# A run-time branch moved from between two passes to the end of the kernel, where it runs a second pass of its own

## The chip, the cores and the metric

The kernel runs on one core of a Trainium2 chip. The metric is the time of one execution on the device in microseconds (us); lower is better. A core has five engines with an instruction stream each: TensorE (PE, matmuls and transposes), VectorE (DVE), ScalarE (ACT), GpSimd (POOL) and SyncE (SP). They meet only through semaphores. In this kernel SP issues the plain transfers between memory and the core, and POOL issues the indirect ones, which gather or scatter rows by a list of row numbers.

## The reference, cut to what matters

Two layers over 64 graphs of 256 nodes with 256 features each (16384 rows in all). The first layer is an attention over the adjacency matrix and a Mamba-2 block; the second is a relational graph convolution and a mixture of eight experts:

```python
x = x + _L0_gnn_ref(_layernorm(x), adj, L0_gnn_W, L0_gnn_a)
x = x + _L0_ffn_ref(_layernorm(x), L0_ffn_W_in, ...)            # Mamba-2
x = x + _L1_gnn_ref(_layernorm(x), L1_gnn_adj, adj, L1_gnn_weight, L1_gnn_bias)
x = x + _L1_ffn_ref(_layernorm(x), L1_ffn_gate_w, ...)          # experts
...
    masks = (relation[None] == rel_ids[:, None, None, None])    # relations 1 to 4
    h = jnp.einsum('rbnm,bmd->rbnd', masks, x)
    y = jnp.einsum('rbnd,rdo->bno', h, weight)
...
    idx = jnp.argmax(probs, axis=-1)                            # one expert per row
    pos = (jnp.cumsum(one_hot, axis=0) * one_hot).sum(-1) - 1   # place in its queue
    kept = pos < C                                              # C = 2560 rows
    hmid = relu(einsum('ecd,edf->ecf', buf, w1) + b1)           # 256 -> 1024
    ybuf = einsum('ecf,efd->ecd', hmid, w2) + b2                # 1024 -> 256
    y = nan_to_num(ybuf[idx, pos_g] * (prb * kept))
```

The adjacency matrix that is given holds only 0 and 1, so of the four relations only the first occurs. The kernel relies on that in its usual form, tests it, and has a general form for other matrices.

## The kernel before, in words

**Pass 1** goes through the graphs two at a time, in 32 groups of 512 rows. Each group does the attention, the Mamba-2 block and the graph convolution, writes its rows to `x3d` in device memory, chooses an expert for every row and scatters a record of four numbers per row (`slots`: row number, probability, and the two numbers of the layer norm) to the place of the row in its expert's queue. The steps of all groups are put in order by a planner written in the kernel (`Plan`), from a cost and a due time for each step, and stand in the program in that order. Two blocks of expert work (`first_block`) are planned into pass 1, to run beside its last groups in homes that the groups no longer need; their last four indirect stores of 128 rows (L1271) are the last work of pass 1.

**The test and the branch.** Each group adds up, on ACT, a number that exceeds a bound if an entry of the matrix is neither 0 nor 1 (`tested`). L1432 to L1438 make of these one whole number, `general`, with two DVE operations, a matmul and a copy. At L1440 every engine loads that number into a register, and at L1444 it enters or jumps over the general form of pass 1: a loop over pairs of groups that does the whole pass again with four relations. With the given data it is jumped over. An engine that jumps over such a block must then count its semaphores as if it had run it; POOL does that for its indirect transfers with an instruction of its own (INC_SWDGE_SEM).

**Pass 2** (`Blocks`, from L1461) does the other expert blocks: first those of 256 rows (the halves, `kind` 1), then those of 512 rows (the wholes, `kind` 0). How many of each there are is known at run time only, so the blocks stand in nested branches (L1602), and an engine leaves the nest after the last block that exists. A block needs its records (`fetch_slots`, SP, L1496), its expert's weights (`fetch_weights`, SP, four transfers, L1505 to L1514), the row numbers as whole numbers (`placed`, two small DVE operations, L1249 and L1250), its rows (`gather`, POOL, one indirect transfer per 128 rows, L1253), the norm (`normed`, DVE, L1259) and the transposes (`turned`, PE and ACT, L1539 and L1542). All this is done a block or two ahead; `experts` then does the two matmuls (L1565, L1575), and DVE, ACT and POOL finish and store the rows. Ahead of the first block `begin` does it for the halves and then for the wholes:

```python
def begin(self):
    for i in range(2):
        self.fetch_slots(i)
    self.fetch_weights(0)
    for i in range(2):
        self.gather(i)
    self.turned(self.norm(0), 0)
...
for blocks in (halves, wholes):
    blocks.begin()
```

So PE, in its own order, transposes the first block of the halves, the first block of the wholes, and then begins the first block of the halves. I call this stretch the prelude.

**Memory.** On-chip memory is given out in pools. `wts` holds pass 1's weights, about 26 KB per partition; `fast` lies above it and holds pass 1's work tiles, those of `first_block` among them. Both are closed before pass 2 opens `et`, `es` and, for PSUM, `eps`, which lie over their bytes. In `et` the homes of a kind come list by list: three of `meta`, of `place`, of `xg`, then two of each other.

Of the kernel before, what the change touches and what calls it, by code (L numbers as in the profile page):

```python
# [19 lines left out]
P = 128  # L20
# [267 lines left out]
def gnn_mamba_rgcn_moe(ctx: ExitStack, tc: tile.TileContext, a: dict, out: bass.AP):  # L288
# [10 lines left out]

    nc = tc.nc  # L300
# [89 lines left out]
    pass1 = ctx.enter_context(ExitStack())  # L390
    wts = pass1.enter_context(tc.tile_pool(name="wts", bufs=1))

    DG, DQ = D + E + 1, D + E + 1 + NH
    DA = DQ + 2
    WX = DA + E + 1 + NH  # L400
    wx = wts.tile([P, 2, WX], F32, name="wx")
    win = wts.tile([P, 2, DPROJ], F32, name="win")
    nc.scalar.dma_start(out=win, in_=a["L0_ffn_W_in"].rearrange("(k p) o -> p k o", p=P))
    wrel = wts.tile([P, 1, 2, DG], F32, name="wrel")
    gb = wts.tile([P, E], F32, name="gb")
    nc.scalar.dma_start(out=gb, in_=row(a["L1_ffn_gate_b"]).broadcast_to([P, E]))
    blin = wts.tile([P, DG], F32, name="blin")
    nc.scalar.dma_start(out=blin[:, 0:D], in_=row(a["L0_ffn_b_lin"]).broadcast_to([P, D]))
    brel = wts.tile([P, DG], F32, name="brel")
    nc.scalar.dma_start(out=brel[:, 0:D], in_=row(a["L1_gnn_bias"]).broadcast_to([P, D]))  # L410
    dtb = wts.tile([P, NH], F32, name="dtb")
    nc.scalar.dma_start(out=dtb, in_=row(a["L0_ffn_dt_bias"]).broadcast_to([P, NH]))
    aneg = wts.tile([P, NH], F32, name="aneg")
    nc.scalar.dma_start(out=aneg, in_=row(a["L0_ffn_A_log"]).broadcast_to([P, NH]))
    nc.scalar.activation(aneg, aneg, AF.Exp)
    nc.vector.tensor_scalar(aneg, aneg, -1.0, None, ALU.mult)
    dch = wts.tile([P, NCT], F32, name="dch")
    dskip = a["L0_ffn_D"].rearrange("(c q) -> q c", q=2)
    for q in range(2):
        nc.scalar.dma_start(  # L420
            out=dch[q * 64 : (q + 1) * 64, :], in_=dskip[q : q + 1, :].broadcast_to([64, NCT])
        )

    cw = wts.tile([P, NCT + 1, 4], F32, name="cw")
    nc.sync.dma_start(out=cw, in_=a["L0_ffn_conv_w"].rearrange("(c p) k -> p c k", p=P))
    nc.vector.tensor_scalar(cw, cw, 0.5, None, ALU.mult)
    cb = wts.tile([P, NCT + 1], F32, name="cb")
    nc.sync.dma_start(out=cb, in_=a["L0_ffn_conv_b"].rearrange("(c p) -> p c", p=P))
    nc.vector.tensor_scalar(cb, cb, 0.5, None, ALU.mult)
    wf = wts.tile([P, NCT, DG], F32, name="wf")  # L430

    gq = wx[:, :, DA:WX]

    def centred(pool, banks, dst, src, n):

        ps = banks.tile([P, 512], F32, tag="ps0", name="ps")
        for k in range(2):
            nc.tensor.matmul(
                ps[:, :n], lhsT=ones_pp, rhs=src[:, k, :], start=(k == 0), stop=(k == 1)
            )  # L440
        for k in range(2):
            nc.vector.scalar_tensor_tensor(
                dst[:, k, :], ps[:, :n], -1.0 / D, src[:, k, :], ALU.mult, ALU.add
            )

    def projected(pool, banks, dst, src, n):

        for k in range(2):
            ps = banks.tile([P, 512], F32, tag="ps0", name="ps")
            for o in range(2):  # L450
                nc.tensor.transpose(
                    ps[:, o * P : (o + 1) * P], src[:, k, o * P : (o + 1) * P], ident
                )
            srcT = pool.tile([P, 2 * P], F32, tag="srcT", name="srcT")
            nc.vector.tensor_copy(srcT, ps[:, : 2 * P])
            ps = banks.tile([P, 512], F32, tag="ps0", name="ps")
            for o in range(2):
                nc.tensor.matmul(
                    ps[:, :n], lhsT=srcT[:, o * P : (o + 1) * P], rhs=gq[:, o, :n],
                    start=(o == 0), stop=(o == 1),  # L460
                )
            nc.vector.tensor_copy(dst[:, k, :], ps[:, :n])

    def relation(pool, banks, dst, r):

        nc.sync.dma_start(
            out=dst[:, :, 0:D], in_=a["L1_gnn_weight"][r].rearrange("(k p) o -> p k o", p=P)
        )
        centred(pool, banks, dst[:, :, 0:D], dst[:, :, 0:D], D)
        projected(pool, banks, dst[:, :, D:DG], dst[:, :, 0:D], E + 1)  # L470

    with tc.tile_pool(name="prep", bufs=1) as prep, tc.tile_pool(
        name="prep_ps", bufs=2, space=PSUM
    ) as prep_ps:
        own = prep, prep_ps

        w0 = prep.tile([P, 2, D], F32, name="w0")
        nc.sync.dma_start(out=w0, in_=a["L0_gnn_W"].rearrange("(k p) o -> p k o", p=P))
        gq0 = prep.tile([P, 2, E + 1 + NH], F32, name="gq0")
        nc.vector.memset(gq0[:, :, E : E + 1], 0.0)  # L480
        nc.sync.dma_start(
            out=gq0[:, :, 0:E], in_=a["L1_ffn_gate_w"].rearrange("(k p) e -> p k e", p=P)
        )
        nc.vector.tensor_copy(gq0[:, :, E + 1 :], win[:, :, DPROJ - NH :])
        centred(*own, gq, gq0, E + 1 + NH)
        nc.vector.memset(gq[:, :, E : E + 1], -1.0 / D)
        centred(*own, wx[:, :, 0:D], w0, D)
        projected(*own, wx[:, :, D:DQ], wx[:, :, 0:D], E + 1 + NH)
        for o in range(0, DPROJ - NH, 512):
            part = win[:, :, o : min(o + 512, DPROJ - NH)]  # L490
            centred(*own, part, part, min(512, DPROJ - NH - o))
        relation(*own, wrel[:, 0], 0)
        for vec, dst in (("L0_ffn_b_lin", blin), ("L1_gnn_bias", brel)):
            col = prep.tile([P, 2], F32, tag="col", name="col", bufs=2)
            nc.sync.dma_start(out=col, in_=a[vec].rearrange("(k p) -> p k", p=P))
            ps = prep_ps.tile([P, 512], F32, tag="ps0", name="ps")
            for k in range(2):
                nc.tensor.matmul(
                    ps[:, : E + 1], lhsT=col[:, k : k + 1].to_broadcast([P, P]),
                    rhs=gq[:, k, : E + 1],  # L500
                    start=(k == 0), stop=(k == 1),
                )
            nc.vector.tensor_copy(dst[:, D:DG], ps[:, : E + 1])

        av = prep.tile([P, 2, D], F32, name="av")
        for i in range(2):
            nc.sync.dma_start(
                out=av[:, i, :],
                in_=a["L0_gnn_a"][i * D : (i + 1) * D, :].rearrange("d o -> o d").broadcast_to([P, D]),
            )  # L510
# [78 lines left out]
    def summed_up(ends):  # L589
        for e in range(1, E):  # L590
            nc.vector.tensor_add(ends[..., e : e + 1], ends[..., e : e + 1], ends[..., e - 1 : e])
# [1048 lines left out]
```

## Time and profile before

| What | Value |
|---|---|
| Median of 9 runs | 2527.13 us (2523.79 to 2534.23) |
| The profiled execution | 2528.44 us, its span 2526.6 us |
| Last matmul of pass 1 ends, first expert matmul of pass 2 begins | 1884.4 us, 1919.8 us |
| PE busy from 1884 to 1920 | 4.7 us (0.42 + 0.67 + 3.57) |
| Mean clock granted to PE, from 1895 to 1920 | 0.50 |
| Last store issued (POOL), end of the span | 2514.6 us, 2526.6 us |

Times in the profile are microseconds from the start of the span. A row of a timeline gives the start, the duration, the engine, the line and the operation, then the tile that is written and those that are read; in brackets stands how long the engine had been idle and what ended that. An engine with a q behind its name (POOLq) is the sequencer of that engine: branches, register loads and waits. Rows with slashes are for all instructions of one kind on a line: shortest, median and longest in ns, then the first and the last start. The releaser in brackets is worked out from semaphores, and where a wait is for several it can be the wrong one.

### The profile page before, as it was taken

The numbers are of one execution on the slowest core, as the hardware profiler recorded it, in microseconds if no ns is written. First come the engines' busy times: TensorE is split into PE (matmuls) and PEld (weight loads), VectorE is DVE, ScalarE is ACT, GpSimd is POOL, SyncE is SP. The second block draws the span as 40 slices with busy tenths as digits, with TensorE's granted clock in tenths as the row PEclk, the third lists the DMA queues.
The fourth block names the chain that finished last, engine by engine and source line by source line (L and its number), as shares of the span: only waits on it lengthen the run. The fifth ranks groups of instructions, "written<-read, shape, count | busy, mean of one in ns | idle before, by whom it ended". The sixth has DMA issues, their size and how long they took to land. (4 is left out here: it accounts for less than half of the span.)

```text
span 2526.6 us, 34990 instructions
## 1 busy us (share of the span) xinstructions
PE 2384.9 (94%) x11489; PEld 1661.8 (66%) x11489; DVE 1921.4 (76%) x4811; ACT 1642.5 (65%) x3712; POOL 832.6 (33%) x756
## 2 busy tenths in 40 slices
PE   5899999999999999999999999999886999999997
PEld 4567766666667666766766676666655666666665
DVE  3899999999989999999999999999752344334433
ACT  1878887878888888888888888786522223322232
POOL 1122424333343433334343333432523222322222
PEclk8999999999999999999999999999997999999999
DMA  3212222322222322222232222231416333333333
GB/s 113 45 23 55 60 61 63 79 56 54 62 54 70 68 66 54 62 53 70 57 75 56 53 62 58 66 62 40 136 38 212 119 109 128 110 124 103 111 124 69
DMA packets 170175, 194.66 MB, mean 77 GB/s; under 512 B 24855, under 2 KB 154975, under 8 KB 169968
## 3 DMA queue, kind: packets, MB, share of 16 engines
q1 hardware_dynamic: 121184, 131.24, 16.6%
q0 software_dynamic: 47104, 59.14, 12.8%
q8 instruction: 97, 1.59, 0.3%
q10 hardware_dynamic: 1680, 1.79, 0.2%
q14 instruction: 110, 0.90, 0.1%
HBM read 108.27 MB, written 45.97 MB: 61 GB/s over the span
## 5 line engine op out<-in xcount | busy, mean ns | idle before, releaser
L697 PE MATMUL ps<-xnT,win 128*128 128x512 f32 x1152 | 544.4, 602 | 4.0 <-ACT xnT L739 4.0
L916 DVE SCALAR_TENSOR_TENSOR y<-ps,cw,y 128x510 f32<-128x510 f32 (+2 forms) x480 | 351.1, 739 | 6.6 <-ACT y L909 5.0
L983 ACT ACTIVATE dm<-ps,cs 128x256 f32<-128x256 f32 (+1 forms) x1024 | 334.5, 477 | 22.8 <-PE ps L697 22.4
L705 POOL TENSOR_TENSOR rs<-ve,mhalf 128x4 f32<-128x4 f32 x96 | 164.4, 1713 | 559.1 <-DVE ve L703 435.8
L697 PEld LDWEIGHTS ps<-xnT,win 128*128 128x128 f32 x1152 | 205.4, 191 | 171.7 <-issue 159.4
L1565 PE MATMUL ps<-xnT,w 128*128 128x512 f32 (+1 forms) x704 | 289.4, 570 | 4.0 <-DMA meta<-slots 4.0
L1575 PE MATMUL ps<-w,hid 128*128 128x256 f32 x1312 | 290.4, 379 | 0.0
L1575 PEld LDWEIGHTS ps<-w,hid 128*128 128x128 f32 x1312 | 247.6, 190 | 40.9 <-issue 9.1
L697 PE MATMUL ps<-wf,gate 128*128 128x265 f32 x1024 | 252.0, 388 | 0.5 <-DVE gate L1061 0.5
L1565 PEld LDWEIGHTS ps<-xnT,w 128*128 128x128 f32 x704 | 136.0, 193 | 146.1 <-issue 133.4
L1041 DVE TENSOR_TENSOR dm<-dm,bc 128x1536 f32<-128x1536 f32 x128 | 225.6, 1764 | 1.7 <-ACT dm L989 0.2
L1569 ACT ACTIVATE hid<-ps,b 128x512 f32<-128x512 f32 (+1 forms) x176 | 115.8, 658 | 166.7 <-PE ps L1565 165.7
L697 PEld LDWEIGHTS ps<-wf,gate 128*128 128x128 f32 x1024 | 191.4, 190 | 48.5 <-issue 11.2
L1580 DVE TENSOR_TENSOR yv<-ps,b 128x256 f32<-128x256 f32 x82 | 34.8, 425 | 237.1 <-PE ps L1575 237.1
L1048 PE MATMUL ps<-dm,xdt 128*64 128x256 f32 x1024 | 169.5, 397 | 33.5 <-DVE dm L1041 33.0
L989 ACT ACTIVATE dm<-dm 128x1536 f32<-128x1536 f32 x128 | 198.6, 1554 | 0.0
L1271 POOL DMA_INDIRECT out_dram<-yf,place x82 | 81.3, 992 | 343.1 <-DVE yf L1588 337.6
L1235 POOL DMA_INDIRECT slots<-meta,sl x128 | 127.9, 1000 | 195.2 <-DVE sl L1232 149.1
L1581 ACT ACTIVATE yv<-yv,meta 128x256 f32<-128x256 f32 x82 | 41.7, 508 | 183.3 <-DVE yv L1580 183.3
L713 DVE BATCH_NORM_STATS2 st<-x 128x6 f32<-128x256 f32 x384 | 151.6, 413 | 7.4 <-DMA x<-in_x_dram 6.8
L922 ACT ACTIVATE xh<-y 128x512 f32<-128x512 f32 x160 | 101.0, 631 | 75.1 <-DVE y L916 66.1
L697 PE MATMUL ps<-wh,eT 128*128 128x273 f32 x512 | 142.6, 407 | 5.6 <-ACT eT L835 4.9
(298 smaller groups left out, 5018.7 us busy)
## 6 DMA issues: line engine op xcount, KB each, us to landing
w<-in_L_ffn_w_dram SPq DMA_DIRECT2D x48, 1024.0 KB
x<-blin POOLq DMA_DIRECT2D x32, 530.0 KB
x<-brel POOLq DMA_DIRECT2D x32, 530.0 KB
adji<-in_adj_dram SPq DMA_DIRECT2D x32, 512.0 KB
x<-in_x_dram SPq DMA_DIRECT2D x32, 512.0 KB
x3d<-x SPq DMA_DIRECT2D x32, 512.0 KB
out_dram<-x SPq DMA_DIRECT2D x32, 512.0 KB
cm<-bm SPq DMA_DIRECT2D x32, 128.0 KB
```

The lines of the kernel that those rows point to most:

```text
L697: nc.tensor.matmul(out_, lhsT=lhsT, rhs=rhs, start=(i == 0), stop=(i == len(pairs) - 1))
L705: s.step(POOL, 1.0, lambda: nc.gpsimd.tensor_tensor(rs(), ve(), mhalf[:, 0:4], ALU.pow), [ve], [rs])
L713: s.step(DVE, 0.34, lambda j=j: nc.vector.bn_stats(sb()[:, j, :], src()[:, j, 0:D]), [(src, j)], [(sb, j)])
L916: nc.vector.scalar_tensor_tensor(y3[:, :, d:], p3[:, :, : N - d], cw[:, c, k : k + 1], y3[:, :, d:], ALU.mult, ALU.add,)
L983: nc.scalar.activation(dm()[:, q, bi, o : o + n], ps()[:, t0 + N - n : t0 + N], AF.Relu, bias=cs()[:, j, h : h + 1], scale=-1.0,)
L989: s.step(ACT, 1.38, lambda: nc.scalar.activation(dm(), dm(), AF.Exp, scale=-1.0), [], [dm])
L1041: s.step(DVE, 1.67, lambda dm=dm: nc.vector.tensor_mul(dm(), dm(), bc().unsqueeze(1).to_broadcast([P, 2, 2, N + P])), [bc], [dm])
L1048: nc.tensor.matmul(o, lhsT=xdt()[:, 2 * bi, h * 64 : (h + 1) * 64], rhs=dm()[:, q, bi, 0:N], start=True, stop=False,)
L1235: s.step(POOL, 1.1, lambda j=j: apart("slots", nc.gpsimd.indirect_dma_start(out=slots, out_offset=bass.IndirectOffsetOnAxis(ap=sl()[:, j : ...
L1565: nc.tensor.matmul(ps[:, :n], lhsT=w1[:, k, f * P : (f + 1) * P], rhs=xnT[:, k, :], start=(k == 0), stop=(k == 1),)
L1569: nc.scalar.activation(hid[:, f, :], ps[:, :n], AF.Relu, bias=self.b1[i % 2][:, f : f + 1])
L1575: nc.tensor.matmul(ps[:, :D], lhsT=hid[:, f, j * P : (j + 1) * P], rhs=w2[:, f, :], start=(f == 0), stop=(f == NFT - 1),)
```

## The change

The two passes become functions of a form, `first_pass(form, pass1)` and `second_pass(form, pass2)`. The usual form (`fast`) runs both without a branch between them. After it every engine loads `general`, and enters or jumps over the general form (`slow`), which now holds the preparation of the weights, the loop, and a second pass of its own. With the given data it is jumped over as before.

In the second pass four things differ. The homes are made block by block: all of the halves' block 0 first, then the other homes of its blocks 1 and 2, then those of the wholes, so that the halves' first homes lie on the bytes of `wts`. The prelude goes step by step over both kinds instead of kind by kind. Its row numbers are written by POOL, not DVE. The four operations that make `general` stand behind the prelude.

```diff
+                kinds = {
+                    "meta": (3, [P, J, 4], F32), "place": (3, [P, 2, J], I32), "xg": (3, [P, J, D], F32),
+                    "w1": (2, [P, 2, F], F32), "w2": (2, [P, NFT, D], F32), "b1": (2, [P, NFT], F32),
+                    "b2": (2, [P, D], F32), "xnT": (2, [P, 2, J * P], F32),
+                }
...
+                for i in range(3):
+                    for name, (n, shape, dtype) in kinds.items():
+                        if i < n:
+                            getattr(self, name).append(et.tile(
+                                shape, dtype, tag=f"{name}{kind}{i}", name=name, bufs=1))
...
-    for blocks in (halves, wholes):
-        blocks.begin()
+        both = (halves, wholes)
+        for blocks in both:
+            for i in range(2):
+                blocks.fetch_slots(i)
+        for blocks in both:
+            for i in range(2):
+                blocks.gather(i, nc.gpsimd)
+        for blocks in both:
+            blocks.fetch_weights(0)
+        for blocks in both:
+            blocks.turned(blocks.norm(0), 0)
+        if form == "fast":
+            other = es.tile([P, NG], F32, tag="yv", name="other")
+            nc.vector.tensor_scalar(other, tested, float(N) + 1.0, None, ALU.is_gt)
+            others = es.tile([P, 1], F32, tag="others", name="others", bufs=1)
+            nc.vector.tensor_reduce(others, other, AX.X, ALU.max)
+            ps = eps.tile([P, 512], F32, tag="ps", name="ps")
+            nc.tensor.matmul(ps[:, 0:1], lhsT=ones_pp, rhs=others, start=True, stop=True)
+            nc.vector.tensor_copy(general, ps[0:1, 0:1])
...
-    again = nc.values_load(
-        general[0:1, 0:1], min_val=0, max_val=P,
-        skip_runtime_bounds_check_because="a count of partitions",
-    )
-    with tc.If(again > 0), ExitStack() as slow:
...
-    pass1.close()
...
+    for form in ("fast", "slow"):
+        with ExitStack() as here:
+            if form == "slow":
+                again = nc.values_load(
+                    general[0:1, 0:1], min_val=0, max_val=P,
+                    skip_runtime_bounds_check_because="a count of partitions",
                 )
+                here.enter_context(tc.If(again > 0))
+            with ExitStack() as pass1:
+                first_pass(form, pass1)
+            with ExitStack() as pass2:
+                second_pass(form, pass2)
```

## The prediction

> **What bounds the kernel now.** I read the share of slices first, then the busy time by stage, then each engine's timeline across the place that changes, then the branch rows.
>
> ```profile
> PE 2384.9 (94%) x11489; PEld 1661.8 (66%) x11489; DVE 1921.4 (76%) x4811; ACT 1642.5 (65%) x3712; POOL 832.6 (33%) x756
> PE   5899999999999999999999999999886999999997
> ```
>
> TensorE is the bound everywhere except at the start, at the seam between the passes (tenths 8, 8, 6) and in the last slice. The branch sits in that seam. The PE timeline there:
>
> ```profile
> 1883.82 0.59 PE L1376 MATMUL ps<-xh,dm 128*128 128x256 f32 x2
> 1907.15 0.66 PE L1539 MATMUL ps<-ident,xn 128*128 128x128 f32 x2 [22.74 <-DMA meta<-slots]
> ...
> 1918.42 1.38 PE L1539 MATMUL ps<-ident,xn 128*128 128x128 f32 x4 [1.20 <-DVE xn L1259]
> 1919.78 5.46 PE L1565 MATMUL ps<-xnT,w 128*128 128x256 f32 x13
> ```
>
> Pass 1's last matmul ends at 1884.4 and the first expert matmul starts at 1919.8: 35.4 us with only twelve transposes. That is all this change can win here. POOL in the same stretch shows what fills it:
>
> ```profile
> 1890.48 0.97 POOL L1271 DMA_INDIRECT out_dram<-y,hide  x1 [1.43 <-DVE y L1390]
> 1898.72 1.01 POOL L1253 DMA_INDIRECT xg<-x3d,place  x1 [7.26 <-DVE place L1250]
> 1900.03 0.97 POOL L1253 DMA_INDIRECT xg<-x3d,place  x1 [0.30 <-issue]
> ...
> 1908.54 0.95 POOL L1253 DMA_INDIRECT xg<-x3d,place  x1 [5.02 <-DVE place L1250]
> ...
> 1912.29 0.94 POOL L1253 DMA_INDIRECT xg<-x3d,place  x1 [0.30 <-issue]
> ```
>
> The last store of pass 1 is issued at 1890.48. Then come the halves' four gathers, a hole of 5.02 us, and the wholes' gathers. The hole is DVE's: it stands in order behind the halves' normalising (first at 1906.43) before it writes the wholes' row numbers at 1908.03. PE has the wholes' transposes ahead of the first block, so the wholes' fourth gather (1912.29) is what releases the start. The rows of the branch itself:
>
> ```profile
> L1444 POOLq EVENT_SEMAPHORE  x5: 17/43/43, 1891.3 to 1893.5; - x5
> L1444 DVEq COMPARE_BRANCH  x1: 72/72/72, 1890.4 to 1890.4; - x1
> L1444 POOLq COMPARE_BRANCH  x1: 53/53/53, 1890.8 to 1890.8; - x1
> L1444 POOLq INC_SWDGE_SEM  x1: 1020/1020/1020, 1893.6 to 1893.6; - x1
> L1444 DVEq EVENT_SEMAPHORE  x1: 21/21/21, 1893.6 to 1893.6; - x1
> ```
>
> DVE's jump took 1890.4 to 1893.6, and POOL saw pass 1's last stores land at 1893.5. SP's first slot fetch follows at 1895.22. So the branch is not alone on this path: the landing of the stores ends at the same moment.
>
> **Does the new pass wait for those stores too?** This decides the sum. Pass 2's tiles lie over two closed pools: the weights (`wrel`'s last matmul is at 1832.8) and the work tiles, whose last reader is the store at 1890.48. The only other place where a pool opens over a closed one is the start:
>
> ```profile
> 42.98 0.38 SPq L549 DMA_DIRECT2D b1d<-b1t  x1
> ...
> 45.35 0.64 POOL L573 MEMSET blank<- 128x640 f32 x1 [40.65 <-DMA b1d<-b1t]
> ```
>
> `blank` is the first tile of the new pool and `b1t` the last of the old one, yet it waited 40.65 us for the landing of `b1t`. A new pool's tile there waited for all users of the pool below, not for those of its own bytes. I take the same for pass 2, over both pools: then the new order of the homes frees nothing early, and all of the prelude still starts at 1893.5.
>
> **The change part by part**, under that reading.
>
> 1. *Branch, its loads and joins out of the seam.* SP no longer waits for DVE's join, loads its register and works through its waits after it: the first slot fetch goes from 1895.22 to about 1893.65, -1.55 us.
> 2. *New prelude order.* SP issues four slot fetches at its old pace (0.85 us apart), so the first weights leave at 1897.0 as they did (1896.94) and cost nothing; by the DMA packets they had landed at about 1906.5, so they are next if the gathers end before that. Row numbers are written by POOL: a POOL copy of 128x8 took 0.25 us (L1190), so a pair 0.5, plus the 0.3 that POOL shows between its own issues. Slot fetch to row numbers took 2.27 (1895.22 to 1897.49). Chain: 1893.65 + 2.27 + 0.8 = 1896.7 first gather; at 1.28 a gather and 0.8 a pair the wholes' fourth is issued at 1896.7 + 7 x 1.28 + 2 x 0.8 - 2 x 0.3 (the gap is in both) = 1906.6, against 1912.29: -5.7, the 1.55 of part 1 included. The four DVE copies removed were idle time.
> 3. *Landing.* Fourth gather to its normalising took 6.35 (1918.64), then 1.14 to the first expert matmul. DMA was full there (share 1.02 from 1908 to 1920), so I keep 6.35. Low bound: were bytes the limit, only the earlier start counts, -1.55. High bound: pass 1's gather landed in 4.85 (issue 1771.33, normalising 1776.18), and -5.7 becomes -7.2; with DVE's price for the row numbers (0.33 a pair) -8. I take -5.7, the row of this very transfer. PE starts at 1914.1, and the rest of pass 2, bound by PE, moves with it. The slow first block (9.56 us where later ones take 7.07, granted clock 0.50 before it) stays, as PE still idles.
> 4. *The test of `general`* (four small instructions) moves from pass 1 into the wait of part 3: nothing. Without that cover, under 1 us. PE's 0.28 at 1869.78 stood beside a wait for ACT.
> 5. *The branch at the end.* PE, ACT, DVE and SP reach it early; POOL is last:
>
> ```profile
> L1602 POOLq EVENT_SEMAPHORE  x4: 17/43/43, 2517.1 to 2517.3; - x4
> ...
> L1602 POOLq COMPARE_BRANCH  x2: 43/46/50, 2514.3 to 2519.1; - x2
> ...
> L1602 POOLq INC_SWDGE_SEM  x1: 1667/1667/1667, 2517.4 to 2517.4; - x1
> ```
>
> Its leaving of the last nest took 2.8 us (2514.3 to 2517.1; DVE's also 2.8), the counter 1.67, and then a drain of 6.24 that ends the kernel. After that nest POOL now loads `general` (0.51 at L1440), jumps over the general form, makes up its semaphores (0.35) and its counter, and only then drains. The jump is unseen: low 0.5 (POOL over the old general form, 1890.8 to 1891.3), high 6.75 (PE's dearest, L1602). The skipped code now holds a whole second pass, as the code left at 2514.3 does, so I take 2.8. Sum 0.51 + 0.05 + 2.8 + 0.35 + 1.67 = +5.4; bounds 2.7 (with 0.5 and a counter of 1.02, and 0.3 for the return) and 9.7.
>
> [...]
>
> **Sum.** -5.7 + 5.4 = -0.3. The profiled execution took 2528.44 (span 2526.6 and 1.84 around it), 1.31 above the median 2527.13; -0.3 on the median is 2526.8. A difference under 0.2% (5.05 us) is about what a measurement of this kernel can't tell from no change.
>
> **Rivals.**
> - *A: a tile waits only for the pool under its own bytes.* The homes of the halves' first block fit over the weights (some 26 KB), so its slots, weights and gathers are done before 1885; SP and DMA are idle enough (34 GB/s from 1850 to 1900). Left after 1893.65 are the wholes' slots and four gathers: 1893.65 + 2.27 + 0.8 + 3 x 1.28 = 1900.6, + 6.35 + 1.14 = 1908.1. Seam -11.7, sum -6.3: 2520.8. For it: the homes are ordered to allow it. Against it: `blank`.
> - *A2: waits by bytes alone.* All of the prelude hides; PE starts at about 1889, after the last PSUM reader (1887.5), at a better clock. Seam -31 - 2.5, sum -28: 2499. Against it: the same row, harder.
> - *B, slower: the end's jump.* Place: POOL, ahead of the 6.24 drain. If it is fetched twice, to the block that makes up semaphores and back, at SP's price for leaving the nest (2484.7 to 2489.6, 4.9), the end costs 0.51 + 9.8 + 0.35 + 1.67 + 0.1 = 12.4, sum +6.7: 2533.8. It turns the sign from an end of 5.7, and passes 0.2% from 10.8. For it: nothing overlaps POOL's end. Against it: POOL's return took 0.4 (2519.1 to the drain at 2519.6).
>
> **How the numbers follow.** Likeliest case 0.58 (bounds: -8 + 2.7 = -5.3 to -1.55 + 9.7 = +8.2, so 2521.8 to 2535.3 of its own): 0.45 within 0.2%, 0.05 faster, 0.08 slower. A 0.19 and A2 0.07, faster. B 0.16: 0.14 slower, 0.02 within. Together faster 0.31, same 0.47, slower 0.22. The range 2516 to 2534.5 takes in A with its error, the likeliest case but its far corner and most of B; A2 and the rest of B, under 0.2, stay out.
>
> **What would show it.** Right: first slot fetch near 1893.6; POOL's gathers in one row with no hole of 5 us; first expert matmul near 1914; POOL's drain 5 us later after its last store than now (2519.6 against 2514.56). Wrong: gathers or weights of pass 2 among pass 1's last stores (A), expert matmuls by 1890 (A2), a gap above 8 us ahead of the drain (B). The prediction also falls if the wholes' fourth gather lands no sooner although issued sooner.

## The result, and the profile after

The kernel after takes 2537.45 us (median of 10 runs, 2531.86 to 2540.56), the kernel before, in 30 runs of the same comparison, 2527.19. The ratio is 1.0037, with a 95% interval of 1.0028 to 1.0046: 10.3 us slower. The prediction was 2526.8 with a range up to 2534.5, so it was wrong, in sign and in range.

The profiled execution of after took 2544.68 us (span 2542.8), 7.2 above its median; that of before 2528.44 (span 2526.6). The first two lines of its page, PE's busy time and PE's tenths in 40 slices:

```profile
PE 2397.0 (94%) x11489; PEld 1669.3 (66%) x11489; DVE 1921.3 (76%) x4803; ACT 1647.2 (65%) x3712; POOL 833.8 (33%) x764
...
PE   5999999999999999999999999999887999999996
```

PE has the same 11489 matmuls as before and is busy 12.1 us longer with them (2397.0 against 2384.9). That can't come from the seam or the tail, where it has almost nothing to do. The PE timeline across the seam (start, duration, line, tiles; in brackets the idle time before and what ended it):

```profile
1893.70 3.19 PE L1377 MATMUL ps<-xh,dm 128*128 128x256 f32 x14
1916.46 0.66 PE L1532 MATMUL ps<-ident,xn 128*128 128x128 f32 x2 [19.57 <-DVE xn L414]
...
1927.06 1.51 PE L1532 MATMUL ps<-ident,xn 128*128 128x128 f32 x4 [0.17 <-DVE xn L414]
1928.76 7.52 PE L1550 MATMUL ps<-xnT,w 128*128 128x256 f32 x26 [0.19 <-issue]
```

Pass 1 ends at 1896.89 instead of 1884.42. From there to the first expert matmul it is 31.87 us instead of 35.36. POOL in that stretch:

```profile
1902.95 0.97 POOL L426 DMA_INDIRECT out_dram<-y,hide  x1 [1.43 <-DVE y L1391]
1908.15 0.19 POOL L404 CAST place<-meta 128x2 int32<-128x2 f32 x1 [4.23 <-DMA meta<-slots]
...
1908.96 1.06 POOL L408 DMA_INDIRECT xg<-x3d,place  x1 [0.40 <-POOL place L405]
...
1912.19 1.02 POOL L408 DMA_INDIRECT xg<-x3d,place  x1 [0.17 <-POOL place L405]
...
1918.58 1.04 POOL L408 DMA_INDIRECT xg<-x3d,place  x1 [0.30 <-issue]
```

The gathers come in one row; the hole of 5.02 us is gone. The wholes' fourth gather leaves 15.63 us after pass 1's last store instead of 21.81. No part of the prelude starts before that store. The rows of the branch at the end (duration of one in ns: minimum, median, maximum; then the starts):

```profile
L1611 POOLq EVENT_SEMAPHORE  x6: 17/30/43, 2533.6 to 2534.0; - x6
...
L1611 POOLq COMPARE_BRANCH  x1: 55/55/55, 2530.6 to 2530.6; - x1
L1611 POOLq INC_SWDGE_SEM  x1: 1647/1647/1647, 2534.1 to 2534.1; - x1
```

POOL jumps at 2530.6, is at the other side at 2533.6, and then adds to its counter; 1.65 later comes a drain of 6.16 us (6.24 in before). From POOL's last store to the last drain, which follows that one and ends the kernel, it is 18.08 us, in before 11.80.

So the span of 2542.8 against 2526.6 divides thus: pass 1's end +12.5, the seam -3.5, pass 2's matmuls +0.9 (592.18 against 591.32), the tail (from the last matmul to the end) +6.3; together +16.2. Seam and tail are what the prediction was about, +2.8 by these two profiles. The 12.5 of pass 1, whose instructions did not change on any engine but for the four that make `general`, it had at nothing.

Where it lies: at 100 us after is 2.6 us early, and then it loses 1.3 to 2.4 us at a time at nine places, one or two pairs of groups (109 us each) apart. At each of these places, and at four others, PE waits 2.2 to 2.6 us for DVE's masked `dm`, in both kernels, thirteen times in pass 1. One of them in before, then the same one in after:

```profile
431.06 0.66 PE L1048 MATMUL ps<-dm,xdt 128*64 128x256 f32 x4 [2.50 <-DVE dm L1041]
...
429.19 0.66 PE L1084 MATMUL ps<-dm,xdt 128*64 128x256 f32 x4 [2.22 <-DVE dm L1077]
```

What follows differs. Three stretches of 3.41 us each of after, with such a gap from 426.97 to 429.19 (length, busy time of PE, PEld, DVE, ACT and POOL, the granted clock, DMA's share, GB/s):

```profile
426.87:430.28 3.41, 1.19 (x13) 1.02 (x14) 3.38 (x5) 1.25 (x5) 2.60 (x1) 1.00 0.00 0
430.28:433.69 3.41, 3.41 (x13) 2.32 (x9) 3.38 (x7) 2.75 (x5) 0.00 (x0) 0.50 0.89 307
433.69:437.11 3.42, 3.42 (x20) 2.39 (x19) 2.68 (x7) 3.05 (x7) 1.01 (x1) 1.00 0.02 5
```

And of before, where the same gap lies from 428.55 to 431.06:

```profile
426.22:429.63 3.41, 2.33 (x10) 1.45 (x8) 2.80 (x7) 2.12 (x7) 0.67 (x2) 1.00 0.01 1
429.63:433.05 3.42, 1.99 (x18) 1.68 (x19) 3.42 (x4) 2.09 (x7) 2.19 (x1) 1.00 0.24 84
433.05:436.46 3.41, 3.41 (x15) 2.49 (x14) 3.33 (x10) 3.41 (x5) 0.13 (x1) 1.00 0.67 228
```

In after the gap lies whole in one stretch (PE busy 1.19 of 3.41) and the next stretch runs at half the clock (0.50). In before it is shared by two stretches (2.33 and 1.99 busy) and the clock stays at 1.00. In the record of the granted clock in these two profiles all falls in pass 1 after 100 us begin on one grid of 3.41 us and last 3.41 or 6.83. I call one a spell, and a stretch of that grid a window. After eleven of the thirteen gaps a spell follows in after, after two in before (the first two expectations below count ten and one of twelve). Over pass 1 from 100 us on that is 47.8 us at half clock against 20.5. Taking half the clock for half the work, the difference would cost 13.7 us if PE were busy in all of it, an estimate from these two lengths; by the rows of after a matmul of 128x292 (L733) took 684 ns in the half-clock stretch above and 409 ns from 440 to 520 us.

Pass 1's matmuls are the same in both kernels, so they can be set side by side one by one. From 300 to 1660 us after falls back by 17.5 us. Of these, 13.1 come just behind the gaps: 1.35 to 1.47 at each of the nine places where after has a spell and before has none, and under 0.2 at each of the other four. Another 5.4 come just ahead of the gaps, 0.7 to 1.2 at each of five places where DVE waited 3.5 us for its inputs to `xdt`, instead of 2.5 to 2.9 as in before; the gaps themselves are 1.0 shorter. So half clock is three quarters of what this execution lost there, and the longer waits are the rest. Ahead of the gap above, DVE's waits in before and then in after:

```profile
424.93 0.69 DVE L1031 TENSOR_TENSOR xdt<-ps,dt 128x512 f32<-128x512 f32 x1 [1.36 <-PE ps L697]
426.37 0.69 DVE L1031 TENSOR_TENSOR xdt<-ps,dt 128x512 f32<-128x512 f32 x1 [0.75 <-PE ps L697]
...
427.83 0.69 DVE L1031 TENSOR_TENSOR xdt<-ps,dt 128x512 f32<-128x512 f32 x1 [0.43 <-PE ps L697]
...
420.74 0.69 DVE L1067 TENSOR_TENSOR xdt<-ps,dt 128x512 f32<-128x512 f32 x1 [0.59 <-PE ps L1062]
423.59 0.69 DVE L1067 TENSOR_TENSOR xdt<-ps,dt 128x512 f32<-128x512 f32 x1 [2.17 <-PE ps L733]
425.03 0.69 DVE L1067 TENSOR_TENSOR xdt<-ps,dt 128x512 f32<-128x512 f32 x1 [0.75 <-remote]
```

How busy PE was in the window ahead of a spell can be read from the profiles of all runs together. From 300 to 1665 us they hold 212 windows at full clock in which PE is busy for less than 2.6 us. All 85 with at most 1.39 us busy are followed by half clock, none of the 109 with 1.58 or more, and 8 of the 18 between (1.49 went both ways). This holds for these gaps only: near 1700 us, where PE does other work, spells also follow windows with up to 2.2 us busy, and no run shows why.

### The profile page after: what moved, and what is told of

The parts are those of the page before. It is cut to its first block, busy times and chain, and to the rows that moved or that the text cites. A ratio compares the mean times of both kernels' runs of the same rounds, so it can differ in the third digit from the quotient of the medians.

```text
span 2542.8 us, 34991 instructions
## 1 busy us (share of the span) xinstructions
PE 2397.0 (94%) x11489; PEld 1669.3 (66%) x11489; DVE 1921.3 (76%) x4803; ACT 1647.2 (65%) x3712; POOL 833.8 (33%) x764
## 3 DMA queue, kind: packets, MB, share of 16 engines
q1 hardware_dynamic: 121184, 131.24, 16.2%
## 5 line engine op out<-in xcount | busy, mean ns | idle before, releaser
L733 PE MATMUL ps<-xnT,win 128*128 128x512 f32 x1152 | 542.1, 600 | 4.0 <-ACT xnT L775 4.0
L741 POOL TENSOR_TENSOR rs<-ve,mhalf 128x4 f32<-128x4 f32 x96 | 155.6, 1622 | 568.5 <-DVE ve L739 445.6
L733 PEld LDWEIGHTS ps<-xnT,win 128*128 128x128 f32 x1152 | 204.7, 190 | 170.8 <-issue 155.4
L733 PE MATMUL ps<-wf,gate 128*128 128x265 f32 x1024 | 252.1, 388 | 0.0
L733 PEld LDWEIGHTS ps<-wf,gate 128*128 128x128 f32 x1024 | 191.6, 190 | 47.9 <-issue 11.2
L733 PE MATMUL ps<-wh,eT 128*128 128x273 f32 x512 | 142.8, 408 | 8.7 <-ACT eT L871 4.9
```

Of the source, the lines that this page charges most:

```text
L733: nc.tensor.matmul(out_, lhsT=lhsT, rhs=rhs, start=(i == 0), stop=(i == len(pairs) - 1))
L741: s.step(POOL, 1.0, lambda: nc.gpsimd.tensor_tensor(rs(), ve(), mhalf[:, 0:4], ALU.pow), [ve], [rs])
```

## The experiments

The runs went to five chips, and these are not equally quick: before took 2486 to 2487 on three (A, B, C), 2544 on one (D) and 2528 on one (E). Times of whole runs are compared on one chip only. Lengths within the seam, the tail and pass 2 are also set beside those of other chips, where they differ little (before's seam took 35.05 to 35.40 us in its four profiles). "The first comparison" is the one above.

### Both kernels again (chip A)

> The kernel before, unchanged, run once more with its own profile. In the profile shown, its granted clock was 0.5 in eight spells after the first 100 us (one of them in twelve at PE's gap of 2.2 to 2.6 us that comes once in every two groups, where PE waits for dm L1041), and pass 1's last matmul ended at 1884.4. Theory W (windows of the clock): pass 1's length varies from run to run with the number of these spells; time 2524 to 2534, and a run with a lower mean clock is the longer one, about 2.2 us for each 0.001. Rival C (the code of the new program itself makes pass 1 longer, through its layout or its fetching): pass 1 of this kernel always ends within 2 us of 1884.4, whatever the clock.

> The kernel after, unchanged, with a second profile. In its first profile the clock was 0.5 in 17 spells after 100 us, ten of them at the twelve gaps of PE in pass 1 (about 3.4 us each), and pass 1's last matmul ended at 1896.9. Theory W: the spells vary, so pass 1 ends anywhere between 1882 and 1898, and the mean clock tells which; median of all near 2537. Rival C: pass 1 ends at 1895 to 1898 again, with a clock that may be anything. Both: the tail stays 5.6 longer than before (counter's start to drain 7.7 against 2.1) and the seam 3 to 4 shorter.

Measured: before against itself 2486.56 and 2486.14, ratio 1.0002 (0.9993 to 1.0012). After 2489.20 (10 runs) against 2486.14 (25 runs): 1.0012 (1.0002 to 1.0022), +3.1 us. Both profiled spans are 2486.9. Pass 1 ends at 1842.24 in before and 1842.32 in after. PE's seam in after:

```profile
1837.62 4.70 PE L1377 MATMUL ps<-xh,dm 128*128 128x256 f32 x21
1861.73 0.66 PE L1532 MATMUL ps<-ident,xn 128*128 128x128 f32 x2 [19.41 <-DVE xn L414]
...
1873.50 2.86 PE L1550 MATMUL ps<-xnT,w 128*128 128x256 f32 x6 [0.15 <-issue]
```

The seam is 31.18 us (before: 35.36), last store to last drain 17.84 (11.74), pass 2's matmuls 591.79 (593.79). Rival C is out: the new program's pass 1 is not longer by itself. But no row of theory W is shown either, since PE has no gap here. Why not is seen at DVE, just ahead of the gap's place, in the first profile of before:

```profile
312.46 0.69 DVE L1031 TENSOR_TENSOR xdt<-ps,dt 128x512 f32<-128x512 f32 x1
314.49 0.69 DVE L1031 TENSOR_TENSOR xdt<-ps,dt 128x512 f32<-128x512 f32 x1 [1.34 <-PE ps L697]
316.64 0.69 DVE L1031 TENSOR_TENSOR xdt<-ps,dt 128x512 f32<-128x512 f32 x1 [1.47 <-remote]
```

and in before on chip A:

```profile
311.81 1.89 DVE L1031 TENSOR_TENSOR xdt<-ps,dt 128x512 f32<-128x512 f32 x3
```

In the first comparison DVE waited 2.8 us here, and 2.5 to 2.9 in the same place of the other pairs of groups, for the semaphore that PE counts up, while PE's own rows there are the same on both chips (16 transposes in 1.91 us, from 311.82 and from 311.18). The profile names PE for the first wait and found no releaser for the second ("remote"). On chip A DVE never waited at this line from 300 to 1660 us. Whether the signals were late, or PE's work behind them later than its rows show, isn't told apart. Between 100 and 1650 us PE is idle 45.5 us in the first profile of before and 12.8 on chip A; most of the 42 us by which pass 1 differs between the two chips is this.

### The general form left out (chip A)

```diff
-    for form in ("fast", "slow"):
+    for form in ("fast",):
```

> After without the general form at the end: neither its branch nor its code is there (it leaves out the form for matrices that the fast form can't take). The tail: 5.6 us less, as counter's start to drain goes from 7.7 back to about 2.1. Theory W: pass 1 as in after, so median 2537.5 - 5.6 = 2531.9, within 3. Rival C, if the long code behind pass 1 is what slows it: pass 1 back at 1884 and the median near 2525.

Measured: 2484.91 (10 runs), 0.9996 of before (0.9987 to 1.0006), 4.3 under after. Last store to last drain is 11.79, as in before (11.74). So the tail is the branch at its end, and worth 6.1 us in the profile. Without it the change would be 1.2 us ahead of before, not measurably faster. The 2531.9 expected was for the chip of the first comparison.

### The gap filled where there is none (chip A)

```diff
-                def heads(c=c, dm=dm, ps=ps):
+                def heads(c=c, dm=dm, ps=ps, fill=fill and c == 0):
+                    for _ in range(3 * fill):
+                        nc.tensor.matmul(ps()[:, 0:N], lhsT=ident, rhs=trif[:, 0:N], start=True, stop=True)
```

> After with three matmuls (128x256 f32, about 1.3 us in all by the rows of 0.43 us) put into PE's gap in pass 1, once in every two groups; they write the bank that the waiting matmuls then overwrite. Theory W: a gap of 2.2 to 2.6 us becomes one of 0.9 to 1.3, no spell at half clock follows it, and pass 1 loses about 1.5 us for each of the ten spells: pass 1 ends near 1881, median 2537.5 - 10 = 2527 (2524 to 2530), mean clock 0.981 or more. Rival C: the gap was idle, filling it changes nothing: 2536 to 2539.

Measured: 2509.10, 19.9 above e2 on the same chip. Neither theory foresaw it, since both took the gap for given. On chip A PE is never idle there, and 15 fills of 1.3 us come on top: PE is busy 2396.1 us instead of 2377.2. Inconclusive for the spells, but it says that pass 1 is bound by PE here to within a few us.

### After again, and the parts of the seam (chip B)

> The kernel after, unchanged, once more beside the kernel before. Where the two ran with PE busy through pass 1 (before at 2486) the seam was 4.2 us shorter (35.36 to 31.18), the way from the last store to the final drain 6.1 longer (11.74 to 17.84), and the median +3.1. In the first pair of profiles (before at 2527) PE had a gap of 2.2 to 2.6 us in every second group of pass 1, and after many of those the clock was at 0.5. Theory W: with PE busy, +2 to +4 and pass 1 of equal length; with the gap there, pass 1 differs too, by the number of spells at half clock, and the median is +5 to +11. Rival C: pass 1 of after is 12 us longer wherever it runs (already against e2).

Measured: 2489.89 against 2487.02, 1.0010 (1.0000 to 1.0019): +2.9 us, with PE busy through pass 1. As on chip A.

```diff
         for blocks in both:
             for i in range(2):
                 blocks.fetch_slots(i)
-        for blocks in both:
+            blocks.fetch_weights(0)
             for i in range(2):
-                blocks.gather(i, nc.gpsimd)
-        for blocks in both:
-            blocks.fetch_weights(0)
-        for blocks in both:
+                blocks.gather(i)
             blocks.turned(blocks.norm(0), 0)
```

> After with the prelude in the order of before: one kind of block after the other, row numbers by DVE. The branch stays at the end. If the new order is worth what the seam shows beyond SP's earlier fetch (4.2 - 1.7), the seam is 2.5 longer than in after, with a hole of 5 us in POOL's gathers, and the time +2.5 against after. By the step of the prediction (wholes' fourth gather 4.1 sooner by the order alone, the landing the same) it would be +4.1. If the order is worth nothing, 0.

Measured: 2491.84, +1.95 against after on the same chip. The seam is 34.06 instead of 31.61, +2.45, and POOL's hole is back:

```profile
1859.01 0.94 POOL L408 DMA_INDIRECT xg<-x3d,place  x1 [0.30 <-issue]
1865.87 0.94 POOL L408 DMA_INDIRECT xg<-x3d,place  x1 [5.92 <-DVE place L405]
```

So of the 3.9 us that the seam lost, the order gives 2.4, and the branch taken out about 1.3 (35.36 for before on chip A to 34.06 here on chip B). The prediction had 4.15 and 1.55.

```diff
-        et = pass2.enter_context(tc.tile_pool(name="et" + form, bufs=2))
+        et = pass2.enter_context(tc.tile_pool(name="et" + form, bufs=2, reuse_waits="tile"))
...
```

(the same for `es` and `eps`)

> After, but the three pools of the second pass let a tile wait only for the users of its own bytes, not for all users of the closed pools under it. Theory P (the prelude waits for the whole of pass 1, last stores included, so the homes' order frees nothing in after): with this the slots, weights and gathers of the halves' first block go out before pass 1's last store, the first expert matmul starts 2 to 6 us after pass 1's last matmul instead of 31, and the time falls by 25 to 29 against after. Rival (something else than the pools' waits holds the prelude: queue order, the slots' landing): first slot fetch still after the last store, no change beyond 2 us.

Measured: 2485.41, 4.5 under after, 0.9994 of before (0.9984 to 1.0003). The first half of theory P holds: SP fetched the slots at 1822.84 and the halves' weights at 1826 to 1828, long before pass 1's last store at 1849.17; in after nothing of the prelude starts before that store. So in after the wait is for the pools' users as a whole. The second half, the 25 us, fell. POOL's timeline of e6 shows why:

```profile
1849.17 0.97 POOL L426 DMA_INDIRECT out_dram<-y,hide  x1 [1.43 <-DVE other L1597]
1850.13 0.20 POOL L404 CAST place<-meta 128x2 int32<-128x2 f32 x1
...
1850.85 1.06 POOL L408 DMA_INDIRECT xg<-x3d,place  x1 [0.28 <-POOL place L405]
```

In POOL's program the gathers stand behind pass 1's last store, and the first of them starts 1.68 us after it, with two operations for its row numbers between; in after it starts 6.01 us after it. So with the pools' wait gone, POOL's own order is what is late next, 4 us earlier.

```diff
-                for i in range(3):
-                    for name, (n, shape, dtype) in kinds.items():
+                for name, (n, shape, dtype) in kinds.items():
+                    for i in range(3):
```

(on top of e6; `xnT` also back to its old place in the list)

> e6 with the homes' order of before (all homes of one name one after the other instead of the first blocks' homes first). Theory P: only here does the order of the homes matter; homes that lie over the last users of pass 1 wait, so the first expert matmul comes later than in e6 by 1 to 25 us. If nothing of the first blocks' homes lies over late bytes in either order: the same as e6 within 1 us.

Measured: 2486.36, against e6's 2485.41; the first expert matmul 21.16 us after pass 1's last store (e6: 21.67). The homes' order does something here: with the old one, the halves' second weights leave at 1846.58 instead of 1827.54. It is worth nothing, since the gathers come later than both. In after, where all homes wait alike, it can't even do that.

### A gap put in (chip C)

```diff
+                def masked(dm=dm, late=late and c == 0):
+                    for n in (N + P,) * 6 * late + (P,) * late:
+                        nc.vector.tensor_mul(spare[:, 0:n], trif[:, 0:n], trif[:, 0:n])
+                    nc.vector.tensor_mul(
+                        dm(), dm(), bc().unsqueeze(1).to_broadcast([P, 2, 2, N + P]))
+
-                s.step(DVE, 1.67, lambda dm=dm: nc.vector.tensor_mul(
-                    dm(), dm(), bc().unsqueeze(1).to_broadcast([P, 2, 2, N + P])), [bc], [dm])
+                s.step(DVE, 1.67, masked, [bc], [dm])
```

> Before, with about 2.8 us of work put on DVE ahead of the masking of dm in every second group of pass 1 (13 times; products of a constant into a spare tile). Where PE was busy through pass 1 it has 0.4 us in hand there, so PE then has a gap of about 2.4 us in every pair of groups, as the first profile of before had. Theory W: +31 for the gaps (13 x 2.4), and on top 0.9 to 1.7 for each spell at half clock that follows one (each lasts 3.4 us), between one spell in thirteen (as the first profile of before) and ten (as the first of after): 2518 to 2535 where before takes 2487. Rival (a gap costs its own time and nothing else): +31 and no spell, 2518.

> After with the same 2.8 us of DVE work. Theory W: what after and before differ by is then the sum of seam and tail (+3) and of the difference in spells at half clock, which may be up to ten x 1.3; if the program's place against the clock's windows is the same from run to run, as the two medians of the first comparison say, +8 to +13 against e9. Rival: +3 against e9, the spells being alike in both.

> e10 with three matmuls (128x256 f32, 1.3 us) in the gap, as in e4. Theory W: the rest of the gap is 1.1 us, no spell at half clock follows, and the time is that of e10 less 0.9 to 1.7 for each of its spells in pass 1, about 2520 where before takes 2487. Rival: filling a gap changes nothing, the same as e10.

Measured, with before at 2487.13 on this chip: e9 2564.87, e10 2566.65, e11 2544.46. The seven products took 3.85 us, more than I had reckoned, and PE's gap is 3.31, in e9:

```profile
427.77 1.08 PE L698 MATMUL ps<-wh,eT 128*128 128x273 f32 x4
432.16 1.13 PE L1054 MATMUL ps<-dm,xdt 128*64 128x256 f32 x4 [3.31 <-DVE dm L1045]
```

The products stand in fourteen places, not thirteen. Thirteen have a gap of 3.31, and the last one, among pass 1's last groups, has 3.65: together 47 us, and the kernel lost 77.7. The rival, that a gap costs its own time alone, is out: after each of the thirteen a spell of 3.41 or 6.83 us follows, in e9 and in e10. e11 fills the gap with 1.3 us of matmuls (rest 1.93), and only three of the thirteen are followed by a spell. It is 22.2 us quicker than e10 although it does more. The mean clock from 100 to 1660 us, e10:

```profile
100.00:1660.00 1560.00, 1506.47 (x7875) 1059.21 (x7875) 1462.83 (x3420) 1267.94 (x2965) 532.07 (x463) 0.98 0.25 58
```

and e11:

```profile
100.00:1660.00 1560.00, 1522.57 (x8074) 1074.42 (x8075) 1479.24 (x3457) 1282.81 (x3002) 538.90 (x468) 1.00 0.26 60
```

0.98 became 1.00. That shows that the gaps bring the spells and that the spells cost time: 58 us fewer at half clock behind these gaps, at most 29 us of PE's work if half the clock is half the work, 22.2 measured. It does not explain the first comparison: between e9 and e10, where every gap has its spell in both, the difference is only 1.8 us, what seam and tail give.

### A gap of the size in question (chip D)

The same edit with five products.

> e9 with less work put in: five products (0.59 each) instead of seven, so PE's gap, 3.31 in e9, becomes about 2.4, the size of the first comparison. At 3.31 every one of the thirteen gaps was followed by a spell at half clock. Theory W: at 2.4 only those are that lie almost whole within one window of 3.41 us; so +31 for the gaps and 2 to 10 spells of 1.7 us each, 2521 to 2535 where before takes 2487, with a spread of 5 us or more between runs (before's own is 4 to 5). Rival: spells after all thirteen, 2540 or more.

> After with the same gap of 2.4 us. If the program of after is what meets more windows (a lasting difference), its median is 8 to 12 above e13 and its mean clock 0.002 lower, as in the first comparison. If the spells fall by chance in both, the medians differ by seam and tail alone: 1 to 4 above e13.

> After again, on whatever chip this is. Before at 2487: +2 to +4, as on the three chips so far. Before at 2527: +5 to +11.

This chip had gaps of its own (before at 2543.70, 2532.60 to 2552.12 in 21 runs), so what was put in came on top of them: they were 4.6 to 5.4 us, longer than a window, and each had its spell in both kernels. e13 took 2597.20, e14 2603.10: +5.9, with five runs each. This does not tell chance from program, the question it was made for. What helps is after itself: 2548.20 against 2543.70, 1.0017 (1.0004 to 1.0029), +4.5 us. In its profile six of the thirteen gaps have a spell. The mean clock of after's runs is 0.9768, of before's 0.9769, so here neither met more spells. In before's 21 runs the clock goes from 0.975 to 0.980, and a straight line through them gives 2.1 us for each 0.001. So the runs of one kernel that spread over 20 us on this chip go with the clock, and so with the spells; where PE has no gap (chips A to C) before's runs spread over 3 to 6 us.

### The landing (chip E)

```diff
-        for blocks in both:
-            blocks.fetch_weights(0)
+        halves.fetch_weights(0)
...
         for blocks in both:
+            if blocks is wholes:
+                blocks.fetch_weights(0)
             with ExitStack() as nest:
```

> After, with the wholes' first weights (2 MB) fetched only between the halves' loop and the wholes' loop, so that the gathers of the prelude share DMA with the halves' weights alone. If sharing is what makes the landing longer: the wholes' fourth gather to the first expert matmul goes from 9.6 back to 7.5 or less, the seam is 2 to 3 us shorter; at the change of kinds up to 5 us come back if the weights are late there. If not: the seam is as in after, within 0.5.

Measured: 2540.40 (5 runs) against 2527.87 (14 runs), 1.0040 (1.0026 to 1.0054). The seam is 31.34, and from the wholes' fourth gather to the first expert matmul it is 9.63 us, as in after (9.5 to 10.2). But the run doesn't test sharing: the halves' next weights move up into the same place. They leave 9.67 us after pass 1's last store, where the wholes' weights left 9.34 after it in the first profile of after, and DMA stays full, with a share of 1.01 from 1921 to 1930. Whether the gathers are held by bytes or by something else is not told apart.

The run shows another thing. Chip E's before is like that of the first comparison (2527.87, there 2527.19), PE's gaps are there, and this relative of after is again 12.5 us behind, with a mean clock of 0.976 against 0.979, eight spells after the thirteen gaps, and pass 1 ending at 1900.27. Its change of kinds costs 2.3 us (PE waits 7.02 us there, in after 4.6 to 4.9, as the wholes' weights come later); seam and tail give 2.5 by the means below; the rest, by subtraction, is pass 1.

### The wholes' transposes behind the halves' loop (chips C, D and E)

On top of e6, the wholes' first normalising and transposes go behind the halves' loop:

```diff
-        for blocks in both:
-            blocks.turned(blocks.norm(0), 0)
+        halves.turned(halves.norm(0), 0)
...
         for blocks in both:
+            if blocks is wholes:
+                blocks.turned(blocks.norm(0), 0)
             with ExitStack() as nest:
```

> e6 (tiles wait for their own bytes alone), and the wholes' first normalising and transposes moved from ahead of the halves' loop to behind it. In e6 POOL's gathers still stood behind pass 1's last store in POOL's order, and PE waited for the wholes' fourth gather (11.3 us after that store) although the halves come first. Expected: PE starts on the halves' second gather (3.05 after the store, + 6.4 landing + 1.1), 10.5 after the store instead of 21.7: -11 in the seam; at the change from halves to wholes 1 to 3 us back, as the transposes are no longer hidden there; against e6 -8 to -10, against before -10. Rival: the weights of the halves, not the gathers, hold the first matmul: then -3 or less.

> e12 again: 8 to 10 us below before (2478 against 2487 in e12), 11 to 13 below after.

Measured: 2478.10 against 2487.13 on chip C, 0.9967 (0.9954 to 0.9979), and 2536.82 against 2543.70 on chip D, 0.9967 (0.9955 to 0.9979): faster than before by 9.0 and 6.9 us, and on chip D 11.4 under after. The move of the transposes alone, with the pools' waits as in after, was not run. PE in e12:

```profile
1837.82 3.83 PE L1377 MATMUL ps<-xh,dm 128*128 128x256 f32 x17
1856.06 0.69 PE L1532 MATMUL ps<-ident,xn 128*128 128x128 f32 x2 [14.41 <-DVE xn L414]
...
1859.86 9.82 PE L1550 MATMUL ps<-xnT,w 128*128 128x256 f32 x32
```

The first expert matmul comes 18.22 us after pass 1's end instead of 31.2 (after on chip A), and 12.16 after its last store (expected 10.5). At the change of kinds 1.6 us come back: PE goes 6.5 us from its last matmul of the halves to the wholes' first, of which 2.1 are the transposes; in e2 it was 4.9.

> e12 with the same later fetch of the wholes' weights. If sharing binds: the first expert matmul less than 10.5 us after pass 1's last store (12.16 in e12), and its first matmuls, 9.82 for 32, back towards 8.5; the change of kinds 0 to 5 longer; in all -3 to +3 against e12. If not: the first matmul at 12.2, and only the change of kinds longer.

Measured: 2523.91 against 2527.87, 0.9986 (0.9971 to 1.0001), so on this chip it isn't shown to be faster than before. The first matmul comes 12.26 after the store (e12: 12.16), and the wait ahead of the wholes' transposes grows from 4.42 to 6.98. The later fetch is of no use. Its pass 1 ends at 1885.46, with spells after four of the thirteen gaps.

## Why the prediction was wrong

**Part 1, branch out of the seam, -1.55.** Right. First slot fetch 3.04 us after pass 1's last store instead of 4.74: -1.70. By the seam of e7 it is worth 1.3.

**Part 2, new order, wholes' fourth gather 5.7 sooner.** Right: 6.18 sooner (15.63 after the last store against 21.81), and no hole.

**Part 3, landing kept at 6.35 + 1.14, first expert matmul at 1914.1 and seam -5.7.** Too much: the seam lost 3.9 us on the mean of eight profiles with after's seam against four with before's (31.4 against 35.3). From the fourth gather to its normalising it was 8.2 instead of 6.35 in the profile on chip A. By e7 the order is what made it longer: with the old one the first expert matmul comes 7.8 us after that gather (7.5 in before), with the new one 9.5 to 10.2. That DMA, full in before already (its share 1.02, which the prediction quotes), brings twelve gathers in one row no quicker is likely and not shown. The prediction had -1.55 as the end "were bytes the limit" and took -5.7, because its row was "of this very transfer". It was, but with fewer gathers beside it. The term is mis-sized by 1.8 us.

**Part 4, test moved, nothing.** Right as far as the runs show; its matmul stands at 1925.82 among transposes that wait for DMA.

**Part 5, branch at the end, +5.4.** The branch itself was right: from the first counter behind the last store to the long drain it is 2.12 us in before and 7.64 on the mean of eight profiles with after's end, +5.5. In the first profile the jump took 2.97 (taken as 2.8), the counter 1.65 (1.67), the load 0.31 (0.51). The term is 1.0 too small all the same: last store to last drain is 11.83 us on the mean in before's four profiles and 18.25 in those eight, +6.4. The rest lies ahead of the branch, where POOL now waits before its first counter: in the first profiles that came 3.66 us after the last store instead of 2.87, and on the means 3.9 instead of 2.9. Rival B, a jump of 9.8, was false: it took 2.97.

**The reading that the prelude waits for both pools whole.** Right, by `blank` as argued; e6 shows it from the other side. Rivals A and A2 were false. A2's 28 us were not to be had even with waits by bytes: POOL's own order holds the gathers, which no rival named.

**Sum, -0.3.** With the terms as measured it is -3.9 + 6.4 = +2.5. On chips A and B after is +3.1 and +2.9, which agrees, on D +4.5. That is within the prediction's range, with the sign wrong by 3 us.

**What put it outside the range** is a term that it did not have. "The rest of pass 2 ... moves with it" and nothing was said of pass 1, that is, 0. That is the step that failed. In the first pair of profiles it was +12.5: 13.1 of half clock behind the gaps and 4.4 of longer waits there, less 2.6 by which after was early at 100 us and 2.5 that it won back between 1660 us and the end of pass 1. By the medians it is about 10.3 - 2.5 = 7.8; this is a subtraction, as only one execution of each kernel was profiled there. Shown: PE has thirteen gaps there on some chips; all 85 windows at such gaps with PE busy 1.39 us or less are followed by half clock, none of the 109 with 1.58 or more; after met eleven such spells in its profile and before two; filling longer gaps in e11 took most spells away. What was known of before had the risk in it: thirteen gaps of PE, a granted clock that fell to 0.5 after two of them, and runs spread over 10 us.

**What stays open.** Why pass 1 took longer in after's runs of the first comparison, with more spells and longer waits in its one profile there, and in a relative of it again on chip E, when its pass 1 has the same instructions; on chip D the mean clocks were equal. The grid of the windows lies elsewhere in each of four profiles: it begins 3.0 us behind a multiple of 3.41 us from the kernel's start in the first profile of before, 0.2 in that of after, 1.1 in e9 and 2.6 in e10. So chance could place one execution, but hardly ten runs (2531.86 to 2540.56) against thirty (2523.79 to 2534.23). What ties these 7.8 us to the change is not known; what the runs trace to it is seam and tail, +2.5. Also open is why DVE waits for PE's semaphore on some chips and not on others.

## What to carry to other kernels

Look for short gaps of a bound PE that come back at a steady interval: each may cost more than its own length (here 1.35 to 1.47 us more where a spell at a clock of 0.50 followed a gap of 2.2 to 2.6 us), and how many do changed from run to run and, in two of the comparisons, with an edit elsewhere, for a reason not found. When a sum comes out near zero, an unlisted term of a few us decides the sign, so give the parts that do not change a bound too. To free a prelude, look for the next thing that holds it: taking away the pools' waits gave 4.5 us against after on chip B, since POOL's order and PE's wait for the second kind's gathers were left, and together with the transposes' move it gave 11.4 against after on chip D. How much of this the move gives alone is open.

## What was not expected of the hardware

- After a gap of 2.22 us in PE's work that lay within one window of 3.41 us the granted clock was 0.50 for the next 3.41 us; after one of 2.50 us that lay across two it stayed at 1.00. At such gaps all 85 windows with PE busy for 1.39 us or less were followed by half clock, and none of the 109 with 1.58 or more.
- DVE waited 1.34 and 1.47 us in a row for the semaphore that PE counts up, with PE's rows as ever, on some chips and not on others. With such waits PE was idle 45.5 us from 100 to 1650 us instead of 12.8, the larger part of a difference of 42 us in pass 1 between chips that run the same program.
- With POOL's last store issued, one more branch at the end cost 6.4 us of an idle core: the load (0.3), a jump of 3.0, a counter of 1.65 and the waits between them, 5.5 in all, and a start of all this that is 1.0 later.
